# Layer norm scales by GpSimd's power, and a rearranged beginning, in a feed-forward, attention, feed-forward kernel

## The chip, the cores and the metric

One core of a Trainium2 chip runs the program. Its engines work side by side, each through its own queue in order: TensorE (PE, with its weight loads as PEld), VectorE (DVE), ScalarE (ACT), GpSimd (POOL) and SyncE (SP), which here issues all DMAs. The metric is the device time of one execution in microseconds (us), lower is better; the number quoted is the median of several runs.

## What is computed

2048 tokens of width 512 pass through a feed-forward, attention with 16 heads of 32, and the same feed-forward again, each behind a layer norm without learned scale and added to its input:

```python
def _layernorm(x, axis=-1, eps=1e-05):
    m = jnp.mean(x, axis=axis, keepdims=True)
    v = jnp.var(x, axis=axis, keepdims=True)
    return (x - m) / jnp.sqrt(v + eps)

x = x + 0.5 * _L0_ffn_ref(_layernorm(x), gate_W_packed, gate_scales, up_W_packed, up_scales, down_W_packed, down_scales)
x = x + _L0_attn_ref(_layernorm(x), w_qkv, b_qkv, w_out, b_out)
x = x + 0.5 * _L0_ffn_ref(_layernorm(x), ...)
```

The feed-forward is `gelu(x Wg) * (x Wu)` times `Wd`, with 4096 hidden units; its weights come as 4-bit codes with a scale for each 32 of them and are dequantized in the kernel. Attention is causal, with a softmax over float32 scores.

## The kernel before

All of `x` lies in SBUF as 16 tiles of 128 tokens by 512 (`xs`), in four blocks of four tiles. A norm belongs to a block (`norm_steps`): on DVE two instructions per tile for the moments (L88, L89); then, for the four tiles at once, the root on ACT (L95), its reciprocal on DVE (L96) and, where ACT normalizes, a bias on DVE (L98). Then tile by tile: the normalization (`xn`) on ACT (L105) or, for the second feed-forward's first two blocks, on DVE (L107); four PE transposes into a PSUM tile (L115); an ACT copy into `xT` (L116). `xn` has two buffers, so a tile waits for the transposes of the one two before it. Twelve norms run: four in each of the three phases.

ACT holds one table of functions at a time. Root, gelu and exp need different ones, so a root among gelus or exps costs a table load ahead of it and one behind it (ACT_TABLE_LOAD in the profile). `root`, a warm-up at the very beginning (L74), loads the root's table.

The order of the instructions is written out by hand; each engine runs its own in program order.

- The beginning (`ffn`, phase 1): SP loads block 0 of `x`, the gate codes and scales, block 1 of `x`, the up codes and scales, then blocks 2 and 3. DVE takes block 0's moments, the gate dequantization (ten steps, L194 to L190), block 1's moments, the up dequantization, and the four token sums (L256 to L259), which need `xT` of blocks 0 and 1. Behind each dequantization POOL makes four sums of the weights (L234 to L237). The products are Strassen-like: seven products of half-size blocks (L276, in the order 1, 2, 6, 7, 5, 4, 3), whose third needs a token sum and a weight sum.
- During the products the next weights are dequantized in the background: `pump` puts two steps behind each product of the first slot (L194 onward). DVE also evacuates most products (L318 to L336), ACT copies two (L315, L327) and applies gelu (L296), POOL adds one pair (L330).
- Blocks 2 and 3 of a feed-forward are normed during the second half of the first group of hidden units, spread over the products by `paced`; the order of PE is product, four transposes, product, and so on. In both feed-forwards this is the same code.
- At the end of the first feed-forward the last down product (L375, `down_pieces`) is mixed with the norm of attention's blocks 0 and 1 (`norms_behind`): first eight POOL sums (`run(fill[0])`, L360 to L363), then a piece of the product, a group of norm steps, a piece, and so on. A piece's results are added to `x` by DVE (L383) and POOL (L389).
- Attention begins with POOL memsets (L542 to L570) and the norms of blocks 2 and 3, mixed with the first projections (L586). Its last pair of heads carries the second feed-forward's norms of blocks 0 and 1, put between the steps by `extra`; there ACT works on exps (L822, L824), DVE on output additions (L628) and reciprocals (L765), POOL on causal masks (L816) and `attnT` (L768).

Of the kernel before, what the change touches and what calls it, by code (L numbers as in the profile page):

```python
# [9 lines left out]
F32 = mybir.dt.float32  # L10
# [4 lines left out]
AF = mybir.ActivationFunctionType  # L15
ALU = mybir.AluOpType
AX = mybir.AxisListType

P = 128
# [5 lines left out]
NB = S // 512  # L25
# [3 lines left out]
EPS = 1e-5  # L29
# [5 lines left out]
def macaron_kernel(ctx: ExitStack, tc: tile.TileContext, x, packed, scales, wqk, bqk, wv, bv, wo, bo, out):  # L35
# [6 lines left out]
    nc = tc.nc  # L42
    PSUM = bass.MemoryType.PSUM

    const = ctx.enter_context(tc.tile_pool(name="const", bufs=1))
# [14 lines left out]
    xs = [xpair[t // 2][:, t % 2, :] for t in range(NT)]  # L60

    def load_x(tb):
        for t in range(4 * tb, 4 * tb + 4):
            nc.sync.dma_start(out=xs[t], in_=x[t * P : (t + 1) * P, :])
# [2 lines left out]

    ident = const.tile([P, P], F32, tag="ident", name="ident")
    make_identity(nc, ident)
    eps = const.tile([P, 1], F32, tag="eps", name="eps")  # L70
    nc.gpsimd.memset(eps, EPS)

    root = const.tile([P, 1], F32, tag="root", name="root")
    nc.scalar.activation(root, eps, AF.Sqrt)  # L74

    def norm_steps(phase, tb, t_out, temp, on_act=False):

        nm = f"{phase}_{tb}"
        mv = small.tile([P, 4, 2], F32, tag="mv", name=f"mv_{nm}")
        rstd = small.tile([P, 4], F32, tag="rstd", name=f"rstd_{nm}")
        nbias = small.tile([P, 4], F32, tag="nbias", name=f"nbias_{nm}")

        def moments(i):
            st = small.tile([P, 6], F32, tag="st", name=f"st_{nm}_{i}")
            nc.vector.bn_stats(out=st, in_=xs[4 * tb + i])  # L88
            nc.vector.bn_aggr(out=mv[:, i, :], in_=st)  # L89

        def stats(i):
            moments(i)
            moments(i + 1)
            if i == 2:
                nc.scalar.activation(rstd, mv[:, :, 1], AF.Sqrt, bias=eps)  # L95
                nc.vector.reciprocal(rstd, rstd)  # L96
                if on_act:
                    nc.vector.scalar_tensor_tensor(nbias, mv[:, :, 0], -1.0, rstd, ALU.mult, ALU.mult)  # L98

        xn = [None] * 4  # L100

        def normalize(i):
            xn[i] = temp(f"xn_{nm}_{i}")
            if on_act:
                nc.scalar.activation(xn[i], xs[4 * tb + i], AF.Identity, bias=nbias[:, i : i + 1], scale=rstd[:, i : i + 1])  # L105
            else:
                nc.vector.tensor_scalar(  # L107
                    xn[i], xs[4 * tb + i], mv[:, i, 0:1], rstd[:, i : i + 1], ALU.subtract, ALU.mult
                )

        def transpose(i):
            xnv = xn[i].rearrange("t (jc p b) -> t jc b p", jc=2, b=2)
            pt = ps_one.tile([P, 4, P], F32, tag="one", name=f"pt_{nm}_{i}")
            for k in range(4):
                nc.tensor.transpose(pt[:, k, :], xnv[:, k // 2, k % 2, :], ident)  # L115
            nc.scalar.copy(t_out[:, :, i * P : (i + 1) * P], pt)  # L116

        steps = [lambda i=i: stats(i) for i in (0, 2)]
        for i in range(5):
            if i < 4:  # L120
                steps.append(lambda i=i: normalize(i))
            if i > 0:
                steps.append(lambda i=i: transpose(i - 1))
        return steps
# [17 lines left out]
    def ffn(phase, finish, behind, loads, ready=(), first_w=None):  # L142
# [8 lines left out]
        with tc.tile_pool(name=f"w{phase}", bufs=1) as wp, tc.tile_pool(name=f"dq{phase}", bufs=1) as dq, tc.tile_pool(  # L151
            name=f"act{phase}", bufs=1
# [94 lines left out]
            xT, xsum = {}, {}  # L247

            def token_sums(tp):
                eng = nc.vector  # L250
                b1, b2 = xT[2 * tp], xT[2 * tp + 1]
                t = xsum[tp] = wp.tile([P, 3, 2, 512], F32, tag=f"xsum{tp}", name=f"xsum_{phase}_{tp}")
                b11, b21, b12, b22 = b1[:, 0:2, :], b1[:, 2:4, :], b2[:, 0:2, :], b2[:, 2:4, :]
                t3, t2, t4 = [t[:, i] for i in range(3)]
                return [
                    lambda: eng.tensor_tensor(t3, b22, b12, ALU.subtract),  # L256
                    lambda: eng.tensor_tensor(b12, b12, b11, ALU.subtract),
                    lambda: eng.tensor_tensor(t2, b22, b12, ALU.subtract),  # L258
                    lambda: eng.tensor_tensor(t4, b21, t2, ALU.subtract),  # L259
                ]  # L260
# [179 lines left out]
            def run(steps):  # L440
                for f in steps:
                    f()
# [4 lines left out]
            for tb in range(NB):  # L447
                xT[tb] = ready[tb] if tb < len(ready) else x_transposed(f"f{phase}", tb)
            norms = [
                norm_steps(f"f{phase}", tb, xT[tb], normed, True) if tb >= len(ready) else [] for tb in range(NB)  # L450
            ]
            rows = Rows(0, 0, first_w)
            second = Rows(0, 1)
            if phase == 1:
                rows.load(0)
                load_x(1)
                rows.load(1)
                load_x(2)
                load_x(3)
                run(norms[0][:2])  # L460
                gate, up = rows.steps(0), rows.steps(1)
                run(gate[:4])
                run(norms[0][2:])
                run(gate[4:])
                run(norms[1][:2])
                run(up[:4])
                run(norms[1][2:])
                run(up[4:10])
                run(token_sums(0))
                run(up[10:])  # L470
                for m in range(2):
                    second.load(m)
                    background += second.steps(m)
                rows.keep()
            else:
                run(token_sums(0))
# [54 lines left out]
    def attention(xT, xT_f, wqk_wv, next_w):  # L531
        with tc.tile_pool(name="aw", bufs=1) as aw, tc.tile_pool(name="qk", bufs=1) as qkp, tc.tile_pool(
# [43 lines left out]
            for tb in (2, 3):  # L576
                xT.append(x_transposed("a", tb))
                norms += norm_steps("a", tb, xT[tb], normed, True)
# [312 lines left out]
            for p in range(NPAIR):  # L891
# [9 lines left out]
                if p + 1 == NPAIR:  # L901

                    o2, o3 = project_out(2), project_out(3)
                    fills = [o2[:4], o2[4:8], o2[8:12] + o3[:4], []]
                    for i in range(4):
                        extra.setdefault(STARTS[3] + 1 + 2 * i, []).append(o3[4 + i])
                    for tb in range(2):
                        xT_f.append(x_transposed("f2", tb))
                        steps = norm_steps(
                            "f2", tb, xT_f[tb], lambda nm: an.tile([P, D], F32, tag="xn", name=nm)  # L910
                        )
                        for i, step in enumerate(steps):
                            extra.setdefault(STARTS[3] + (2 + i if tb == 0 else 9 + i // 2), []).append(step)
# [61 lines left out]
    def load_first():  # L975
        early["ffn"] = weights("w_2_0_0")
        nc.sync.dma_start(out=early["ffn"], in_=kept[0, 0])

    ffn(1, lambda *_: None, norms_behind, load_qkv)
    attention(xT_a, xT_f, early["qkv"], load_first)  # L980

    def store_out(t, half, x_):

        rows = out[t * P : (t + 2) * P, half * 256 : half * 256 + 256]
        nc.sync.dma_start(out=rows.rearrange("(j p) n -> p j n", p=P), in_=x_)

    ffn(2, store_out, lambda temp: [], lambda: None, xT_f, early["ffn"])


# [62 lines left out]
```

## Time and profile before

| | |
|---|---|
| runs of the kernel | median 3295.95 us of 3 (3295.63, 3295.95, 3298.71) |
| the profiled execution | 3300.15 us, of which the span is 3298.4 us |
| PE busy | 3249.1 us (99%) |
| DVE, ACT, POOL busy | 2043.7 (62%), 872.9 (26%), 1128.3 us (34%) |
| table loads on ACT | 17, of 1.28 us each |
| roots on ACT (L95) | 12, of 0.30 us each |
| reciprocals and biases on DVE (L96, L98) | 12 of 0.18 us and 10 of some 0.16 us |
| normalizations on ACT (L105) | 40, of 0.81 us each |

The profile comes from one execution. Times in the prediction are from the start of its span. A row of a timeline gives the start, the duration (from the first to the last where several are merged), engine, line, operation, output and inputs, shapes, the count, and in brackets how long the engine stood idle before it and whose instruction ended that. In a list of waits each row gives the waiting instructions, whom they waited for, the total, how often, and the longest. Windows give the busy time of each engine in a stretch of the span, and then the clock that was granted to PE as a share of its full clock.

### The profile page before, as it was taken

The numbers are of one execution on the slowest core, as the hardware profiler recorded it, in microseconds if no ns is written. First come the engines' busy times: TensorE is split into PE (matmuls) and PEld (weight loads), VectorE is DVE, ScalarE is ACT, GpSimd is POOL, SyncE is SP. The second block draws the span as 40 slices with busy tenths as digits, with TensorE's granted clock in tenths as the row PEclk, the third lists the DMA queues.
The fourth block names the chain that finished last, engine by engine and source line by source line (L and its number), as shares of the span: only waits on it lengthen the run. The fifth ranks groups of instructions, "written<-read, shape, count | busy, mean of one in ns | idle before, by whom it ended". The sixth has DMA issues, their size and how long they took to land.

```text
span 3298.4 us, 34148 instructions
## 1 busy us (share of the span) xinstructions
PE 3249.1 (99%) x12656; PEld 1723.4 (52%) x12656; DVE 2043.7 (62%) x3152; ACT 872.9 (26%) x1802; POOL 1128.3 (34%) x1319
## 2 busy tenths in 40 slices
PE   7999999999999999999999999999999999999999
PEld 3556565655656565333344333346565565656556
DVE  7877777877777556565655664554455455545545
ACT  4111111111111131554544455431111111111111
POOL 2546464554646341322212223113132221313222
PEclk9999999999999999999999999999999999999999
DMA  3111111111111100000000000100011101011101
GB/s 134 54 65 64 64 47 66 67 48 68 64 64 46 70 17 7 6 15 6 14 3 8 29 21 8 48 23 31 37 45 45 45 23 45 27 41 45 45 23 51
DMA packets 42055, 134.15 MB, mean 41 GB/s; under 512 B 5864, under 2 KB 26344, under 8 KB 35360
## 3 DMA queue, kind: packets, MB, share of 16 engines
q1 hardware_dynamic: 41888, 131.96, 11.0%
q8 instruction: 100, 1.64, 0.2%
q14 instruction: 67, 0.55, 0.1%
HBM read 81.91 MB, written 48.46 MB: 40 GB/s over the span
## 4 chain that ended last, share of the span: by engine, by line
PE 94%; DVE 3%; ACT 2%; issue 1%; POOL 0%; DMA 0%; SPq 0%; POOLq 0%; DVEq 0%; ACTq 0%
PE po L375 23%; PE pu L276 23%; PE pg L276 22%; PE av L729 8%; PE pm L668 6%; PE pqk L586 3%; PE ps L790 2%; PE pp L625 2%; PE pv L603 2%; PE ps L799 2%; ACT pt L822 1%; DVE st_f L88 0%; PE pt_f L115 0%; PE pt_a L115 0%; DVE parts L683 0%
## 5 line engine op out<-in xcount | busy, mean ns | idle before, releaser
L375 PE MATMUL po<-wd,inter 128*128 128x256 f32 x2048 | 484.0, 380 | 0.0
L276 PE MATMUL pg<-xT_f,w 128*128 128x512 f32 x1024 | 479.6, 596 | 0.0
L276 PE MATMUL pu<-xT_f,w 128*128 128x512 f32 x1024 | 476.0, 592 | 0.0
L375 PEld LDWEIGHTS po<-wd,inter 128*128 128x128 f32 x2048 | 389.9, 191 | 155.5 <-issue 104.3
L683 DVE TENSOR_REDUCE parts<-pm 128x1 f32<-128x512 f32 (+3 forms) x640 | 370.9, 608 | 155.0 <-PE pm L668 145.3
L330 POOL TENSOR_TENSOR u<-u,u 128x512 f32<-128x512 f32 x128 | 163.4, 1276 | 865.8 <-ACT u L327 861.5
L389 POOL TENSOR_TENSOR x<-x,d 128x512 f32<-128x512 f32 x248 | 329.7, 1340 | 344.7 <-DVE d L383 170.8
L276 PE MATMUL pg<-xsum,w 128*128 128x512 f32 x768 | 357.4, 595 | 5.2 <-DVE xsum L258 3.2
L375 PE MATMUL po<-wd,s 128*128 128x256 f32 x1536 | 362.2, 379 | 0.0
L276 PE MATMUL pu<-xsum,w 128*128 128x512 f32 x768 | 355.7, 592 | 0.0
L375 PEld LDWEIGHTS po<-wd,s 128*128 128x128 f32 x1536 | 291.5, 190 | 116.2 <-issue 79.2
L668 PE MATMUL pm<-kT,qT 32*128 32x512 f32 (+3 forms) x1280 | 333.9, 574 | 0.5 <-DVE parts L683 0.4
L729 PE MATMUL av<-pt,vaug 128*64 128x512 f32 (+3 forms) x1280 | 304.2, 559 | 4.2 <-ACT both L738 1.9
L822 ACT ACTIVATE pt<-ps 128x512 f32<-128x512 f32 (+3 forms) x576 | 271.5, 532 | 137.4 <-PE ps L799 135.5
L276 PEld LDWEIGHTS pg<-xT_f,w 128*128 128x128 f32 x1024 | 195.8, 192 | 194.6 <-issue 180.9
L276 PEld LDWEIGHTS pu<-xT_f,w 128*128 128x128 f32 x1024 | 194.0, 190 | 189.9 <-issue 180.3
L799 PE MATMUL ps<-qT,kT 32*128 32x512 f32 (+3 forms) x1280 | 277.5, 534 | 0.0
L276 PEld LDWEIGHTS pg<-xsum,w 128*128 128x128 f32 x768 | 146.2, 191 | 152.9 <-issue 140.9
L276 PEld LDWEIGHTS pu<-xsum,w 128*128 128x128 f32 x768 | 145.5, 190 | 142.4 <-issue 135.4
L383 DVE SCALAR_TENSOR_TENSOR x<-po,x 128x512 f32<-128x512 f32 x192 | 131.5, 685 | 115.7 <-ACT d L397 85.9
L816 POOL TENSOR_SCALAR_AFFINE_SELECT pt<-pt 128x256 f32<-128x256 f32 x128 | 52.1, 407 | 388.0 <-ACT pt L815 387.8
L383 DVE SCALAR_TENSOR_TENSOR d<-po,d 128x512 f32<-128x512 f32 x192 | 131.8, 686 | 83.4 <-PE po L375 82.6
(128 smaller groups left out, 3603.6 us busy)
## 6 DMA issues: line engine op xcount, KB each, us to landing
kept<-wd SPq DMA_DIRECT2D x8, 1792.0 KB
wd<-kept SPq DMA_DIRECT2D x8, 1792.0 KB
x<-in_x SPq DMA_DIRECT2D x16, 256.0 KB
pk<-in_gate_codes SPq DMA_DIRECT2D x16, 256.0 KB
sc<-in_gate_scales SPq DMA_DIRECT2D x32, 128.0 KB
pk<-in_up_codes SPq DMA_DIRECT2D x16, 256.0 KB
sc<-in_up_scales SPq DMA_DIRECT2D x32, 128.0 KB
pk<-in_down_codes SPq DMA_DIRECT2D x16, 256.0 KB
```

Source lines behind the costliest of these rows:

```text
L276: nc.tensor.matmul(ps, lhsT=a[:, j, :], rhs=b[:, j, :], start=(j == 0), stop=(j == 1))
L330: nc.gpsimd.tensor_tensor(u4, u4, u2, ALU.add)
L375: nc.tensor.matmul(ps[:, j, :], lhsT=a[i][:, k, bass.ts(2 * q + j, P)], rhs=b[i][:, k, :], start=(k == 0), stop=(k == 1),)
L383: stt(dst, ps, 0.5, other, ALU.mult, ALU.add)
L389: adder.tensor_tensor(dst, dst, other, ALU.add)
L586: nc.tensor.matmul(ps, lhsT=w[:, j, k, :], rhs=xT[tb][:, k, :], start=(k == 0), stop=(k == 3))
L603: nc.tensor.matmul(ps[:, i, :], lhsT=xT[t // 4][:, k, (t % 4) * P : (t % 4 + 1) * P], rhs=wv_sb[:, k, bass.ts(half, 256)], start=(k == 0), ...
L668: nc.tensor.matmul(ps[a][:, :n], lhsT=q[r, bass.ts(4 * g + i, P)], rhs=k[r, kb * 512 : kb * 512 + n], start=True, stop=not on_pe,)
L683: nc.vector.tensor_reduce(parts[:, a, i, kb : kb + 1], ps[a][:, :n], AX.X, ALU.max)
L729: nc.tensor.matmul(av[64 * a : 64 * a + 64, off:], lhsT=vaug[:, c, p % 4, HD * a : HD * a + 2 * HD], rhs=pt[:, a, off:], start=(c == 0), s ...
L799: nc.tensor.matmul(ps[a][:, off:], lhsT=k[r, bass.ts(c, P)], rhs=q[r, g * 512 + off : (g + 1) * 512], start=False, stop=True,)
L822: nc.scalar.activation(pt[:, a, plain:], ps[a][:, plain:], AF.Exp, scale=scale)
```

## The change

The root on ACT and the reciprocal and bias on DVE become four operations on POOL: variance plus epsilon, that to the power -0.5 (against a constant tile `expo`), the mean times -1, and that times the scale. Where DVE normalizes, only the first two. `eps`, `root` and its warm-up go. For blocks 0 and 1 of the first feed-forward tiles 1 and 3 are normalized on POOL, with one instruction of two scalars from a tile, tiles 0 and 2 still on ACT. In the beginning block 1 of `x` is loaded ahead of the gate codes; the moments and scales of both blocks come first, then both blocks' normalizations and transposes, then the gate dequantization, the token sums and the up dequantization.

```diff
-    eps = const.tile([P, 1], F32, tag="eps", name="eps")
-    nc.gpsimd.memset(eps, EPS)
-    root = const.tile([P, 1], F32, tag="root", name="root")
-    nc.scalar.activation(root, eps, AF.Sqrt)
-    def norm_steps(phase, tb, t_out, temp, on_act=False):
+    expo = const.tile([P, 4], F32, tag="expo", name="expo")
+    nc.gpsimd.memset(expo, -0.5)
+    def norm_steps(phase, tb, t_out, temp, on_act=False, on_pool=()):
...
             if i == 2:
-                nc.scalar.activation(rstd, mv[:, :, 1], AF.Sqrt, bias=eps)
-                nc.vector.reciprocal(rstd, rstd)
+                nc.gpsimd.tensor_scalar(rstd, mv[:, :, 1], EPS, None, ALU.add)
+                nc.gpsimd.tensor_tensor(rstd, rstd, expo, ALU.pow)
                 if on_act:
-                    nc.vector.scalar_tensor_tensor(nbias, mv[:, :, 0], -1.0, rstd, ALU.mult, ALU.mult)
+                    nc.gpsimd.tensor_scalar(nbias, mv[:, :, 0], -1.0, None, ALU.mult)
+                    nc.gpsimd.tensor_tensor(nbias, nbias, rstd, ALU.mult)
...
             xn[i] = temp(f"xn_{nm}_{i}")
-            if on_act:
+            if i in on_pool:
+                nc.gpsimd.tensor_scalar(
+                    xn[i], xs[4 * tb + i], rstd[:, i : i + 1], nbias[:, i : i + 1], ALU.mult, ALU.add
+                )
+            elif on_act:
                 nc.scalar.activation(xn[i], xs[4 * tb + i], AF.Identity, bias=nbias[:, i : i + 1], scale=rstd[:, i : i + 1])
...
-                norm_steps(f"f{phase}", tb, xT[tb], normed, True) if tb >= len(ready) else [] for tb in range(NB)
+                norm_steps(f"f{phase}", tb, xT[tb], normed, True, (1, 3) if tb < 2 else ())
+                if tb >= len(ready) else []
+                for tb in range(NB)
...
             if phase == 1:
+                load_x(1)
                 rows.load(0)
-                load_x(1)
                 rows.load(1)
                 load_x(2)
                 load_x(3)
-                run(norms[0][:2])
                 gate, up = rows.steps(0), rows.steps(1)
-                run(gate[:4])
-                run(norms[0][2:])
-                run(gate[4:])
-                run(norms[1][:2])
-                run(up[:4])
-                run(norms[1][2:])
-                run(up[4:10])
-                run(token_sums(0))
-                run(up[10:])
+                run(norms[0][:2] + norms[1][:2] + norms[0][2:] + norms[1][2:])
+                run(gate + token_sums(0) + up)
```

## The prediction

> **What bounds the kernel now.** I read the page's chain first: PE holds 94% of it, so only microseconds in which PE stands still, or runs at half clock, can be won or lost. The waits of PE say for whom it stands:
>
> ```profile
> engine line waited for: us in total, times, longest us
> PE pt_f L115 <- ACT xn_f L105: 24.8, 6, 9.6
> PE ps L790 <- ACT pt L822: 4.5, 4, 2.6
> PE pg L276 <- DVE xsum L258: 3.2, 3, 1.3
> PE pt_a L115 <- ACT xn_a L105: 3.0, 2, 2.8
> ```
>
> All but the third are layer norm (the second is an exp queued behind a root). So I took the timelines around the six places where a norm runs: the start; blocks 2, 3 of the first feed-forward (60 us); attention's blocks 0, 1 (1180 us) and 2, 3 (1210 us); the second feed-forward's 0, 1 (2080 us) and 2, 3 (2160 us). From PE's:
>
> ```profile
> 65.66 1.13 PE L115 MATMUL pt_f<-ident,xn_f 128*128 128x128 f32 x4 [4.95 <-ACT xn_f L105]
> ...
> 1181.87 0.77 PE L115 MATMUL pt_a<-ident,xn_a 128*128 128x128 f32 x4 [2.79 <-ACT xn_a L105]
> ...
> 1209.80 0.63 PE L115 MATMUL pt_a<-ident,xn_a 128*128 128x128 f32 x4
> ...
> 2082.12 0.86 PE L790 MATMUL ps<-wo_bo,ones_b 3*128 3x512 bf16 x2 [2.63 <-ACT pt L822]
> ...
> 2163.99 1.13 PE L115 MATMUL pt_f<-ident,xn_f 128*128 128x128 f32 x4 [4.29 <-ACT xn_f L105]
> ```
>
> The bracket is what PE lost. The windows of DVE, then of all engines (fifth pair of columns POOL, then the clock):
>
> ```profile
> 24.80:65.30 40.50, 38.62 (x65) 0.97 0.33 128
> ```
> ```profile
> 2124.80:2126.90 2.10, 0.12 (x2) 0.07 (x1) 2.03 (x3) 0.41 (x1) 0.00 (x0) 1.00 1.00 430
> ...
> 2127.90:2131.30 3.40, 3.40 (x6) 1.34 (x5) 1.42 (x3) 0.63 (x1) 0.00 (x0) 0.51 1.00 430
> ```
>
> The first: from the token sums until block 3's bias DVE works 38.62 of 40.5 us, so DVE, not PE (which runs dry at 60.7), sets when block 2's norm comes. The others: a stop of PE of 2.0 us is followed by 3.4 us at half clock, a loss of 1.7.
>
> **The change.** It removes 12 roots, the `root` warm-up and 13 of 17 table loads (1.28 us each) from ACT, 12 reciprocals and 10 `nbias` from DVE, and four normalizations from ACT; POOL gets 44 tiny operations and those four. Each norm waits for a POOL chain of four (two for `xT_f` blocks 0, 1). POOL's tiny two-input operation (L697, 128x8) takes 0.21 us, the cast L694 0.22; a power is not in this trace. Bounds: 0.21, and 1.34 (the mean 128x512 addition, L389). I take 0.3, near the tiny row: a chain is 0.22+0.3+0.22+0.21 and gaps of 0.06, 1.1 us (1.0 to 2.2). A one-input 128x512 on POOL: affine selects take 0.29 at 128x128, 0.407 at 128x256, so 0.64 by extension; bounds 0.52 (memset of 128x512) and 1.34. I take 0.7.
>
> *Start and blocks 2, 3 of the first feed-forward.* Three transfers (codes, two scales) go behind four of `x` on SP; 1 MB at the 295 GB/s of 2 to 4 us is 3.6 us, and the codes are now wanted at 11.3 instead of 8.5 us, so this hides. DVE does block 1's four moments right behind block 0's (7.88 + 4 x 0.8 and some landing = 11.3). On POOL both chains stand ahead of the first normalization, so it waits for block 1's moments: 12.5 us. Two buffers then make a zigzag: POOL 0.7, transposes 0.75, POOL 0.7, transposes 0.75, copy 0.6, ACT 0.8, transposes 0.7, copy 0.6, ACT 0.8, two transposes 1.35, copy 0.6, with some 0.9 of hops: the sums can begin at 21.75 instead of 24.82. But the dequantization of `up` (as 8.54 to 14.44: 5.9 us) now follows the sums: 21.75 + 4 x 1.23 + 0.3 for POOL's clashes + 5.9 = 32.9, where DVE reached the background work at 31.02 before. That is 1.9 late. POOL's sums of `up` move onto DVE's background work (about 0.5 more); block 2's root, reciprocal and bias (58.99 to 59.76) go: -0.8. L329, which feeds the gelu ahead of block 2's normalization on ACT, starts at 61.98+1.6 = 63.6; 0.69 + 0.63 + 0.80 and hops bring the transposes to 65.9, against 65.66. ACT without four table loads saves some 0.4 in the next two. PE, 3 us earlier into the first product, only waits longer. Term: -0.2 (-2 to +3 by the bounds above).
>
> *Attention 0, 1.* POOL takes everything in order, and there the changed kernel's order has eight sums and an addition ahead of the chain:
>
> ```profile
> 1181.02 1.51 ACT L105 ACTIVATE xn_a<-x,nbias_a,rstd_a 128x512 f32<-128x512 f32 x2
> ```
> ```profile
> 1182.14 1.27 POOL L363 TENSOR_TENSOR s<-inter,s 128x512 f32<-128x512 f32 x1
> 1183.37 1.71 POOL L389 TENSOR_TENSOR x<-x,d 128x512 f32<-128x512 f32 x1
> ```
>
> The moments are ready at 1176.2; POOL is free at 1183.41+1.34 = 1184.75, the chain ends at 1185.85, ACT's 0.81 brings the transposes to 1186.75 instead of 1181.87: +4.9 (4.5 to 6). Behind PE's waiting transposes stand all later pieces of the down product; nothing covers it. The half clock after the stop (1182.4 to 1185.8, 0.51) is there in both.
>
> *Attention 2, 3.* The chain stands behind 16 memsets:
>
> ```profile
> 1206.75 2.40 POOL L570 MEMSET vaug<- 128x128 f32 x16
> ```
>
> They end at 1209.15; with 1.1 and 0.81 the transposes come at 1211.2 instead of 1209.80: +1.4. A new stop may bring half a clock: 1.7 at one chance in three, +0.5. Term +1.9 (1 to 3.1). Here the page "TensorE: Matmul & The Clock Gate", section "HAM oscillation", speaks of idle gaps above some 3.4 us only; the 2.0 us stop above disagrees. By that rule this half microsecond would fall away and the sum would be -1.8.
>
> *Second feed-forward 0, 1, inside attention.* ACT's queue holds exps behind a root that waits for moments:
>
> ```profile
> 2074.36 1.28 ACT L95 ACT_TABLE_LOAD   x1
> 2079.87 0.30 ACT L95 ACTIVATE rstd_f<-mv_f,eps 128x4 f32<-128x4 f32 x1 [4.22 <-DVE mv_f L89]
> 2080.18 1.28 ACT L822 ACT_TABLE_LOAD   x1
> ```
>
> Without it PE's 2.63 and the half clock behind it (2083.5 to 2087.0, 0.51: 1.7) go: -4.3. POOL's two operations end at 2080.5, hidden by DVE's L765; but the next output piece then waits some 0.7 for POOL's `attnT`. At block 1 ACT's 0.23 and 0.17 go, and perhaps half of another 1.7: -1.0; DVE's 0.92 stays (0.55 for root and reciprocal, 0.65 for POOL's pair). Term -4.6 (-6.5 to -2.5).
>
> *Second feed-forward 2, 3.* DVE is not full there. Moments end at 2157.3, POOL's chain at 2158.5; L329, without the reciprocal's 0.76, at 2159.55; 0.69+0.63+0.80 and hops: transposes at 2161.7 instead of 2163.99, -2.3. The slow stretch of 4.9 us (clock 0.50) shrinks to one of 3.4: -0.7, and the next transposes wait 0.3 less. Term -3.3 (-4.7 to -1.5).
>
> **Sum.** -0.2+4.9+1.9-4.6-3.3 = -1.3 us. The profiled execution spans 3298.4 (3300.15 with what lies around it), so it would span 3297.1; the runs' median is 4.2 below it, 3295.95, and I put the same difference on it: 3294.6. Elementwise work belongs on VectorE by the page "GPSIMD Engine Reference", section 4.1, which calls one-input work on GpSimd roughly line rate; its 769 ns for 512 elements (section 3.1) would add an estimated 0.1 to the sum.
>
> **Rivals.** A measurement of this kernel can tell about 0.2%, 6.6 us.
> (1) Slower: the power is dear on POOL. The chain lies open at the start (through DVE's queue), at 1185, at 1210 and twice near 2090; at 2158 it has 2 us of cover. Each microsecond above 1.1 costs 5, and from 2.7 us per chain (7.9/5 more) it decides. At 3 us: -1.3+9.5 = +8.2, 3304. For it: no row shows a power. Against: four columns only, and POOL's tiny rows take 0.2.
> (2) Faster: DVE gives way, because its 38.62 us hold clashes with POOL (L202 1.64 instead of 0.69) that the new order dissolves; then the 3.1 us at the start stay (-3.7 with the reciprocal), and the shorter stops end the half clock at 60 and 2160 us: 2 x 1.7. -1.3-3.7-3.4 = -8.4, 3287.5. Against: POOL gets more work in just that stretch.
> (3) The table loads were covered: in the second feed-forward the next wait takes half of the 7.9 back; +2.6, 3298.6. For it: PE's 0.92 for DVE and `attnT` are near.
> (4) It doesn't do what it says: four table loads stay, by the changed kernel's own order, so a root is left nowhere; no chance given.
>
> **How the numbers follow.** Forecast 0.71, (1) 0.11, (2) 0.12, (3) 0.06. The terms' ends added are -7.7 and +8.1, all at once unlikely; the range of 8 in 10 reaches 3288 to 3302. Beyond 6.6 us lie most of (1) and (2) and a little of the forecast's own ends: faster 0.13, within 0.77, slower 0.10.
>
> **What would show it.** The first token sum (DVE `xsum`) near 21.7 and the first transposes of `xn_f` block 2 near 66 us: the DVE step. PE's wait for `xn_a` near 7.7 us, its longest after the start's and block 2's: the POOL step. No `ps` wait for ACT near 2080, and the block 2 stop of the second feed-forward near 2 us. Wrong if POOL's power takes over 1.5 us, or if `xn_a` waits under 4.

## The result, and the profile after

Run by turns with the kernel before on one chip, the changed kernel takes 3303.24 us in the median of 14 runs (3300.27 to 3305.55), the one before 3297.44 of 14 (3294.49 to 3300.43). The ratio is 1.0017 (95% interval 1.0010 to 1.0024): 5.8 us slower, inside the 0.2% named as the bound and just outside the predicted range (3288 to 3302), on the other side of "before" than the forecast. Of the 8.6 us by which it misses the 3294.6 forecast, 1.5 are the base: the forecast stood on a median before of three runs, 3295.95. Against before, -1.3 was forecast. The profiled execution after took 3303.2 us (span 3301.3).

Below are the waits of PE in the profile after: waiting instruction, whom it waited for, us in total, how often, the longest.

```profile
engine line waited for: us in total, times, longest us
PE pt_f L117 <- ACT xn_f L107: 23.6, 5, 11.1
PE pt_a L117 <- ACT xn_a L107: 11.2, 3, 8.9
PE pt_f L117 <- POOL xn_f L103: 4.0, 2, 3.5
...
PE pt_f L117 <- DVE xn_f L109: 2.1, 2, 1.8
PE ps L787 <- ACT pt L819: 1.4, 1, 1.4
```

The exp's wait (`ps`, 4.5 us in four) has shrunk to 1.4, attention's wait (`pt_a`, 3.0) has grown to 11.2. The single stops, from PE's timeline after (start, duration, engine, line, operation, in brackets the idle time before):

```profile
69.97 1.13 PE L117 MATMUL pt_f<-ident,xn_f 128*128 128x128 f32 x4 [8.69 <-ACT xn_f L107]
...
1192.72 1.13 PE L117 MATMUL pt_a<-ident,xn_a 128*128 128x128 f32 x4 [8.89 <-ACT xn_a L107]
...
1224.03 0.74 PE L117 MATMUL pt_a<-ident,xn_a 128*128 128x128 f32 x4 [2.12 <-ACT xn_a L107]
...
2106.81 0.72 PE L117 MATMUL pt_f<-ident,xn_f 128*128 128x128 f32 x4 [1.82 <-DVE xn_f L109]
...
2167.34 0.75 PE L117 MATMUL pt_f<-ident,xn_f 128*128 128x128 f32 x4 [1.91 <-ACT xn_f L107]
```

So the losses sit at the first feed-forward's block 2 (8.69 against 4.95) and at attention's block 0 (8.89 against 2.79), the gains in the second feed-forward. The operation that no row showed before, from the costliest groups of instructions (busy us, mean ns of one):

```profile
L93 POOL TENSOR_TENSOR rstd_f<-rstd_f,expo 128x4 f32<-128x4 f32 x8 | 8.8, 1094 | 0.7
...
L93 POOL TENSOR_TENSOR rstd_a<-rstd_a,expo 128x4 f32<-128x4 f32 x4 | 4.2, 1039 | 0.3
L103 POOL TENSOR_SCALAR xn_f<-x,rstd_f,nbias_f 128x512 f32<-128x512 f32 x4 | 3.9, 987 | 5.3 <-PE pt_f L117 2.7 <-issue 2.6
```

A power of four columns costs 1.04 us, not 0.3; a normalization on POOL 0.99 in the mean, not 0.7. The timeline of POOL at the start, after, shows both, and their order:

```profile
11.40 0.31 POOL L92 TENSOR_SCALAR rstd_f<-mv_f 128x4 f32<-128x4 f32 x1 [1.22 <-DVE mv_f L86]
11.80 1.47 POOL L93 TENSOR_TENSOR rstd_f<-rstd_f,expo 128x4 f32<-128x4 f32 x1
13.33 0.64 POOL L95 TENSOR_SCALAR nbias_f<-mv_f 128x4 f32<-128x4 f32 x1
14.05 0.34 POOL L96 TENSOR_TENSOR nbias_f<-nbias_f,rstd_f 128x4 f32<-128x4 f32 x1
14.38 1.27 POOL L103 TENSOR_SCALAR xn_f<-x,rstd_f,nbias_f 128x512 f32<-128x512 f32 x1
17.01 1.15 POOL L103 TENSOR_SCALAR xn_f<-x,rstd_f,nbias_f 128x512 f32<-128x512 f32 x1 [1.36 <-PE pt_f L117]
19.50 0.77 POOL L103 TENSOR_SCALAR xn_f<-x,rstd_f,nbias_f 128x512 f32<-128x512 f32 x1 [1.34 <-PE pt_f L117]
```

Block 1's chain takes 3.0 us while DVE dequantizes (until 17.5), 1.92 where DVE leaves POOL alone; only then comes block 0's tile 1 on POOL (14.38). DVE, before and then after:

```profile
24.82 1.27 DVE L256 TENSOR_TENSOR xsum<-xT_f 128x1024 f32<-128x1024 f32 x1 [0.61 <-ACT xT_f L116]
...
31.02 0.41 DVE L194 TENSOR_SCALAR mag<-pk 128x512 uint32<-128x512 uint32 x1
```
```profile
25.54 1.47 DVE L258 TENSOR_TENSOR xsum<-xT_f 128x1024 f32<-128x1024 f32 x1 [8.03 <-ACT xT_f L118]
...
31.12 0.42 DVE L196 TENSOR_SCALAR mag<-pk 128x512 uint32<-128x512 uint32 x1
...
36.94 0.42 DVE L196 TENSOR_SCALAR mag<-pk 128x512 uint32<-128x512 uint32 x1
```

After the change DVE stands idle for 8.03 us before the first token sum, then still has the `up` dequantization (31.12) to do, and reaches the background work at 36.94, against 31.02 before. And POOL ahead of attention's norm, after:

```profile
1188.55 1.26 POOL L391 TENSOR_TENSOR x<-x,d 128x512 f32<-128x512 f32 x1
1189.90 0.23 POOL L92 TENSOR_SCALAR rstd_a<-mv_a 128x4 f32<-128x4 f32 x1
1190.20 1.04 POOL L93 TENSOR_TENSOR rstd_a<-rstd_a,expo 128x4 f32<-128x4 f32 x1
1191.31 0.23 POOL L95 TENSOR_SCALAR nbias_a<-mv_a 128x4 f32<-128x4 f32 x1
1191.62 0.20 POOL L96 TENSOR_TENSOR nbias_a<-nbias_a,rstd_a 128x4 f32<-128x4 f32 x1
```

The chain stands behind POOL's last addition, without a gap: it waits for its turn, not for its data (DVE's last moments of this block end at 1181).

### The profile page after: what moved, and what is told of

It is laid out like the page before. It is cut to its first block, busy times and chain, and to the rows that moved or that the text cites. A ratio compares the mean times of both kernels' runs of the same rounds, so it can differ in the third digit from the quotient of the medians.

```text
span 3301.3 us, 34144 instructions
## 1 busy us (share of the span) xinstructions
PE 3242.5 (98%) x12656; PEld 1722.5 (52%) x12656; DVE 2037.6 (62%) x3130; ACT 848.9 (26%) x1772; POOL 1152.7 (35%) x1367
## 3 DMA queue, kind: packets, MB, share of 16 engines
q8 instruction: 100, 1.64, 0.2%
## 4 chain that ended last, share of the span: by engine, by line
PE 94%; DVE 2%; POOL 1%; ACT 1%; issue 1%; DMA 0%; POOLq 0%; SPq 0%; DVEq 0%; ACTq 0%
PE pu L278 23%; PE pg L278 23%; PE po L377 23%; PE av L726 8%; PE pm L665 6%; PE pqk L583 3%; PE ps L787 2%; PE pp L622 2%; PE pv L600 2%; PE ps L796 2%; ACT pt L819 1%; PE pt_f L117 0%; DVE st_f L85 0%; DVE parts L680 0%; PE pt_a L117 0%
```

## The experiments

The theory before the runs: the new beginning costs several microseconds by itself, because DVE gets through the start later; in attention the order of POOL's sums costs as much; the power only its own microsecond where it lies open. The rival: it is the power. The median of each run against the kernel before on its own chip (3297.21 us of 33 runs for the first four, 3297.93 of 27 for the others):

| kernel | median us | against before | ratio, 95% |
|---|---|---|---|
| old_beginning | 3294.97 | -2.2 | 0.9993 (0.9984 to 1.0002) |
| new_beginning_root | 3302.46 | +5.3 | 1.0016 (1.0007 to 1.0025) |
| cheap_power | 3295.53 | -1.7 | 0.9996 (0.9987 to 1.0004) |
| sums_split | 3296.87 | -0.3 | 1.0000 (0.9991 to 1.0009) |
| no_pool_norm | 3299.78 | +1.9 | 1.0007 (0.9998 to 1.0016) |
| sums_last | 3298.83 | +0.9 | 1.0003 (0.9995 to 1.0012) |
| moments_first | 3296.08 | -1.9 | 0.9994 (0.9985 to 1.0003) |
| best | 3284.37 | -13.6 | 0.9960 (0.9948 to 0.9973) |

Against before, only new_beginning_root and best are clear of noise; the other six intervals contain 1. Against the changed kernel (1.0010 to 1.0024), old_beginning, cheap_power, sums_split, moments_first and best are clear of it. What no_pool_norm and sums_last show rests on their profiles alone.

Microseconds of this size are better read by stage. From PE's timeline of each profiled execution I took where five marks lie and subtracted: S1 from the start to the first gate product (`pg`) behind block 3's transposes, S2 from there to attention's first projection (`pqk`), S3 to its first score maximum (`pm`), S4 to the first product of the second feed-forward, S5 to its first gate product behind block 3's transposes. The rest is 1114.4 us in all. Differences to before; the last column is DVE's reaching the background work, then the start of block 2's transposes:

| kernel | S1 | S2 | S3 | S4 | S5 | DVE free, transposes |
|---|---|---|---|---|---|---|
| before, us | 85.46 | 1117.47 | 15.70 | 902.66 | 62.67 | 31.02, 65.66 |
| after | +4.75 | +7.20 | +2.40 | -8.62 | -2.75 | 36.94, 69.97 |
| old_beginning | -3.60 | +7.14 | +2.41 | -8.56 | -2.74 | 31.32, 63.96 |
| new_beginning_root | +4.53 | -0.02 | 0.00 | -2.20 | -0.73 | 34.59, 70.01 |
| cheap_power | +3.07 | +5.93 | +1.55 | -9.50 | -4.48 | 36.27, 69.31 |
| sums_split | +3.52 | +1.95 | +2.41 | -8.60 | -2.77 | 36.75, 69.79 |
| no_pool_norm | -0.13 | +6.45 | +4.11 | -7.08 | -4.45 | 32.95, 66.00 |
| sums_last | -2.32 | +6.64 | +4.10 | -7.20 | -2.77 | 32.67, 65.24 |
| moments_first | -4.55 | +6.65 | +4.11 | -6.91 | -4.43 | 30.66, 63.00 |
| best | -2.21 | -3.63 | +2.54 | -8.65 | -2.75 | 31.85, 63.87 |

A stretch of half clock is 3.4 us long or a multiple of it, and 3.4 us of it cost up to 1.7. Before's profiled execution has one at 1418.0 us that no other of the first five has, so about 1.7 of each S4 there is not the change's. No_pool_norm, sums_last and moments_first have one in S3 and one near 1425: that is the 1.4 to 1.7 by which their S3 and S4 lie above after's. Where S5 is -4.4 or -4.5, after's stretch at 2133.8 or at 2168.0 is absent. Each kernel has one profiled execution, and where such a stretch falls differs from one to the next (last section): differences of 1.7 us or less in a single stage are weak evidence.

**old_beginning.** The power stays; loads, order and engines of the beginning as before.

```diff
-                norm_steps(f"f{phase}", tb, xT[tb], normed, True, (1, 3) if tb < 2 else ())
+                norm_steps(f"f{phase}", tb, xT[tb], normed, True, ())
...
+                rows.load(0)
                 load_x(1)
-                rows.load(0)
                 rows.load(1)
...
+                run(norms[0][:2])
                 gate, up = rows.steps(0), rows.steps(1)
-                run(norms[0][:2] + norms[1][:2] + norms[0][2:] + norms[1][2:])
-                run(gate + token_sums(0) + up)
+                run(gate[:4])
+                run(norms[0][2:])
+                run(gate[4:])
+                run(norms[1][:2])
+                run(up[:4])
+                run(norms[1][2:])
+                run(up[4:10])
+                run(token_sums(0))
+                run(up[10:])
```

> The power stays on GpSimd in every norm; the beginning alone is as before (loads, order, all normalizations on ScalarE). Theory: the loss of the first 90 us (+4.8) is the order, the token sums ahead of the up dequantization, so that VectorE stands idle 8 us. Then block 2's transposes of the first feed-forward come near 64 us (before 65.7, changed 70.0) and the time is 6 to 7 us below the changed kernel, near 3297. Rival: the power of 1.04 us in each norm is the loss; then the beginning gains at most 2 and the time stays above 3301.

Measured -2.2 us against before where after has +5.8: the new beginning costs 8. In the stages it is S1 alone (-3.60 against +4.75). From its PE timeline:

```profile
63.96 0.74 PE L117 MATMUL pt_f<-ident,xn_f 128*128 128x128 f32 x4 [1.92 <-ACT xn_f L107]
```

The stop is 1.92 us instead of 8.69, and no half clock follows it. It came 2 us below the expected 3297; the 10.2 us of half clock behind block 2 in after are gone too.

**new_beginning_root.** The new beginning and its POOL tiles, the scales by root, reciprocal and bias as before.

```diff
-                nc.gpsimd.tensor_scalar(rstd, mv[:, :, 1], EPS, None, ALU.add)
-                nc.gpsimd.tensor_tensor(rstd, rstd, expo, ALU.pow)
+                nc.scalar.activation(rstd, mv[:, :, 1], AF.Sqrt, bias=eps)
+                nc.vector.reciprocal(rstd, rstd)
                 if on_act:
-                    nc.gpsimd.tensor_scalar(nbias, mv[:, :, 0], -1.0, None, ALU.mult)
-                    nc.gpsimd.tensor_tensor(nbias, nbias, rstd, ALU.mult)
+                    nc.vector.scalar_tensor_tensor(nbias, mv[:, :, 0], -1.0, rstd, ALU.mult, ALU.mult)
```

> The other half alone: the new beginning, with two tiles per block normalized by GpSimd, but root, reciprocal and bias where they were before. Theory: the beginning's loss of 4 to 5 us stays (block 2's transposes near 69), attention's blocks 0, 1 go back to a stop of 2.8 us and its blocks 2, 3 to none, the stop at the exps of 2.6 us comes back: about 4 above before, near 3301.5. Rival (the power is the loss at the start too): within 1.5 of before.

+5.3 us, S1 +4.53: the beginning loses without any power in it. S2 and S3 stand at zero: what attention loses is the chain of four on POOL. The token sums, from DVE's timeline of this run, begin 2.2 us earlier than in the changed kernel, and still 1.6 behind the 21.75 of the prediction:

```profile
23.35 1.73 DVE L260 TENSOR_TENSOR xsum<-xT_f 128x1024 f32<-128x1024 f32 x1 [4.74 <-ACT xT_f L120]
```

**cheap_power.** A product in place of the power; the kernel leaves out the true scale, so only its times can be read.

```diff
-                nc.gpsimd.tensor_tensor(rstd, rstd, expo, ALU.pow)
+                nc.gpsimd.tensor_tensor(rstd, rstd, expo, ALU.mult)
```

> The changed kernel with the power replaced by a multiplication of the same two tiles: the scale is not computed, so the output is not the reference's. It prices the power by itself. Each chain falls from 1.95 to about 1.1, which is what was forecast for it. Theory: 1.2 us back at the start, 0.8 at 1190, 0.8 at 1221, 1 in the second feed-forward's blocks 0, 1, nothing in its blocks 2, 3: 3.8 in all, near 3299.4. Rival (only the power was mis-sized, everything else of the forecast holds): 8 back, near 3295.

-1.7 us, 7.5 below after: by the time alone the rival's number. By the rows only part of it is direct. One of its products on POOL, then the stop of PE at attention's block 0:

```profile
1188.54 0.20 POOL L93 TENSOR_TENSOR rstd_a<-rstd_a,expo 128x4 f32<-128x4 f32 x1
```
```profile
1190.21 1.13 PE L117 MATMUL pt_a<-ident,xn_a 128*128 128x128 f32 x4 [8.05 <-ACT xn_a L107]
```

The product takes 0.20 us for 1.04, and where the chain lies open the wait shrinks by about that: block 2's transposes come 0.66 earlier, attention's stop falls from 8.89 to 8.05, S3 by 0.85, the wait for DVE in the second feed-forward's block 1 from 1.82 to 0.98; 3.2 us. The profiled execution is 6.4 us shorter than after's (span 3294.9). Of the other 3.2, some 2.7 are half clock behind stops that are no shorter than after's: behind block 2 (8.69 us in both) 6.8 us of it are left of 10.2, and the stretch at 2133.8, behind a stop of 1.98 in after and 1.99 here, is absent. So the cheap product doesn't show that the power costs 7.5. And the token sums, on DVE, still start late:

```profile
25.12 1.23 DVE L258 TENSOR_TENSOR xsum<-xT_f 128x1024 f32<-128x1024 f32 x1 [8.28 <-ACT xT_f L118]
```

DVE idles even longer (8.28 us): little of the beginning's delay is the power's.

**sums_split.** Half of the eight sums behind the scales of attention's blocks 0 and 1.

```diff
-            run(fill[0])
+            run(fill[0][:4])
             groups = behind(normed)
+            if phase == 1:
+                groups[3] += fill[0][4:]
```

> The changed kernel, but the last four of GpSimd's eight sums at the end of the first feed-forward are issued behind the scales of attention's blocks 0 and 1 instead of ahead of them. Theory: the stop of 8.9 us there is the queue of sums ahead of the chain; it falls to about 3.2, the slow clock behind it gets shorter by 1, and the time falls by 6 to 7, near 3296.5. Rival: the later down pieces wait for the moved sums instead, and less than 3 comes back.

-0.3 us, 6.1 below after. S2 falls from +7.20 to +1.95; that S1 falls too, by 1.2, is a shorter stretch of half clock behind block 2 (6.8 us, not 10.2), ahead of the edit. PE's timeline:

```profile
1186.18 1.13 PE L117 MATMUL pt_a<-ident,xn_a 128*128 128x128 f32 x4 [3.58 <-ACT xn_a L107]
```

The stop shrinks by 5.31, close to four sums of POOL (4 x 1.35, start to start); the half clock behind it does not (PE works 6.0 us at half speed after the stop; in after 5.9, from 1192.72 to 1198.6). So the order of the sums is a second loss, separate from the beginning's.

**no_pool_norm** and **sums_last** take the beginning apart: all tiles on ACT, and the `up` dequantization ahead of the token sums.

```diff
-                norm_steps(f"f{phase}", tb, xT[tb], normed, True, (1, 3) if tb < 2 else ())
+                norm_steps(f"f{phase}", tb, xT[tb], normed, True, ())
```
```diff
-                run(gate + token_sums(0) + up)
+                run(gate + up[:10] + token_sums(0) + up[10:])
```

> The changed kernel with all normalizations of the beginning on ScalarE again (GpSimd keeps the scales). Theory: GpSimd's 1.27 and 1.15 us under VectorE's dequantization and the zigzag through two buffers hold the token sums back; they come near 23 instead of 25.5 us, the beginning loses some 2 instead of 4.75, near 3300. Rival: the order alone is the loss and ScalarE's turn is as long; then the sums come at 25 or later and nothing changes.

> The changed kernel with one move: the up dequantization ahead of the token sums, where VectorE stood idle for 8 us. Theory: VectorE reaches the background work near 31 instead of 36.9 us and is not behind; block 2's transposes come near 64 instead of 70, the beginning ends 6 earlier, near 3296.5. Rival: the token sums are late anyway and PE's wait for the third product eats it; less than 2.

From DVE's timeline of no_pool_norm, and then of sums_last:

```profile
22.20 1.23 DVE L258 TENSOR_TENSOR xsum<-xT_f 128x1024 f32<-128x1024 f32 x1 [5.09 <-ACT xT_f L118]
...
32.95 0.42 DVE L196 TENSOR_SCALAR mag<-pk 128x512 uint32<-128x512 uint32 x1
```
```profile
26.20 1.55 DVE L258 TENSOR_TENSOR xsum<-xT_f 128x1024 f32<-128x1024 f32 x1 [2.39 <-ACT xT_f L118]
...
32.67 0.94 DVE L196 TENSOR_SCALAR mag<-pk 128x512 uint32<-128x512 uint32 x1
```

Without POOL's normalizations the sums start 3.3 us earlier, though the slow chain of block 1 is still there (11.24 to 14.39): ACT has block 0's tiles to do meanwhile. With the `up` dequantization ahead, the idle 8.03 become 2.39. Either way DVE is free some 4 us earlier, and the transposes of block 2 come 4.0 and 4.7 earlier. Sums_last came out 2.3 us above its number, which the two stretches of half clock (S3, S4) more than explain; its transposes came at 65.24, not at 64.

**moments_first.** Both edits; what is left of the new beginning is the loads and the moments first.

> Both of these together: the moments of both blocks first, all normalizations on ScalarE, up dequantization ahead of the token sums. Theory: they add, to a point: token sums near 23, block 2's transposes near 62, near 3294.5. Rival: one of them makes the other worthless, within 1 of the run with the sums last.

-1.9 us, 1.6 above the number, again with the two stretches. S1 is -4.55, the best of all; with up's dequantization ahead DVE no longer stands idle for the sums, which start at 24.52. DVE is free at 30.66, so the two savings (3.99 and 4.27) overlap: together 6.28.

**best.** old_beginning, with the sums four by four behind the scales of attention's blocks 0 and 1, and the `vaug` memsets behind the norms of blocks 2 and 3.

```diff
-            run(fill[0])
             groups = behind(normed)
+            if phase == 1:
+                groups[1] += fill[0][:4]
+                groups[3] += fill[0][4:]
+            else:
+                run(fill[0])
...
-            for t in range(NT):
-                nc.gpsimd.memset(vaug[:, t, :, HD : 2 * HD], 1.0)
...
+            for t in range(NT):
+                nc.gpsimd.memset(vaug[:, t, :, HD : 2 * HD], 1.0)
             fill = qk[4:6] + v[:2] + qk[6:8] + v[2:]
```

> The power on GpSimd in all norms with the beginning of before, and two moves of what GpSimd has queued: of the eight sums at the end of the first feed-forward four go behind the scale of attention's block 0 and four behind that of block 1, and the memsets of vaug go behind the norms of its blocks 2 and 3. Theory: the beginning 3.6 below before, the stop of 2.8 at attention's blocks 0, 1 falls to under 0.5 and its slow clock goes (-4), blocks 2, 3 lose 1.1 instead of 2.4, the second feed-forward's 9 stay: 14 to 15 below before, near 3283. Rival: the moved sums stop the later pieces by as much as they free, and it ends at old_beginning's 3295.

3284.37 us (five runs, 3282.47 to 3285.97), ratio 0.9960 (0.9948 to 0.9973): below both kernels, and 10.6 below old_beginning, which differs in the two moves alone; S2 goes from +7.14 to -3.63. PE's timeline, then POOL's:

```profile
1176.96 0.74 PE L117 MATMUL pt_a<-ident,xn_a 128*128 128x128 f32 x4
...
1180.37 1.99 PE L377 MATMUL po<-wd,s 128*128 128x256 f32 x8 [0.47 <-POOL s L364]
...
1206.37 0.74 PE L117 MATMUL pt_a<-ident,xn_a 128*128 128x128 f32 x4 [2.25 <-ACT xn_a L107]
```
```profile
1174.12 0.23 POOL L92 TENSOR_SCALAR rstd_a<-mv_a 128x4 f32<-128x4 f32 x1 [0.28 <-DVE mv_a L86]
1174.43 1.04 POOL L93 TENSOR_TENSOR rstd_a<-rstd_a,expo 128x4 f32<-128x4 f32 x1
...
1203.52 0.23 POOL L92 TENSOR_SCALAR rstd_a<-mv_a 128x4 f32<-128x4 f32 x1 [1.69 <-DVE mv_a L86]
```

The stop at attention's start is gone and with it the half clock; the price is 0.47 us for a sum that comes late. The memsets' move was a miss: the chain now waits for DVE's moments (1.69) and the stop is 2.25 instead of 2.12. S1 came at -2.21, not at the expected -3.6, with one stretch of half clock at 64.7 that old_beginning hasn't. The beginning of moments_first together with this order was not tried.

## Why the prediction was wrong

The terms, each as predicted and as the stages show it:

| term | predicted | measured |
|---|---|---|
| start and blocks 2, 3 of the first feed-forward | -0.2 (-2 to +3) | +4.75 |
| attention 0, 1 | +4.9 (4.5 to 6) | +7.2 |
| attention 2, 3 | +1.9 (1 to 3.1) | +2.4 |
| second feed-forward 0, 1 | -4.6 (-6.5 to -2.5) | -8.6, some -6.9 without before's stretch at 1418 |
| second feed-forward 2, 3 | -3.3 (-4.7 to -1.5) | -2.75 |
| sum | -1.3 | +3.0, some +4.7 without that stretch |

**The step that failed** is "Two buffers then make a zigzag ... the sums can begin at 21.75": they began at 25.54. Of the 3.8 us late, 1.9 lie ahead of POOL's first normalization (14.38, not 12.5: block 1's chain took 3.0 us, not 1.1), 1.0 in the two of its normalizations that the zigzag counts (1.27 and 1.15 for 0.7 each), the remaining 0.9 in transposes, copies and hops. The runs agree: the sums begin at 23.35 with the chains off POOL, at 22.20 with the normalizations off it, at 25.12 with the power alone made cheap. I had seen that POOL takes both chains first and had priced chain and tiles as if POOL were alone, although my own figures had DVE dequantizing at that time. The step after it held: from the token sums to the background work 11.4 us, worked out as 11.15. So did "DVE, not PE, sets when block 2's norm comes": block 2's transposes follow 32.0 to 33.1 us behind DVE's being free in the eight kernels without roots, and 34.6 and 35.4 in the two with them. The prediction's own numbers (65.9 and 32.9) put 33.0 there, and after has 33.03. So the root's removal gave what was worked out for it, 1.6 us, and the whole miss of the transposes (69.97 for 65.9) is the 5.9 us by which DVE came late instead of 1.9. "PE, 3 us earlier into the first product" fell with the same step: that product came at 24.73, and at 23.96 before. The longer stop then brought 10.2 us of half clock instead of 6.8, some 0.8 of the term (5.6 us of work at half speed instead of 4.0).

**The power was mis-sized**: 1.04 us, not 0.3, a chain of 1.92 instead of 1.1. "Near the tiny row" was the wrong choice between the bounds 0.21 and 1.34. Rival (1) named this mechanism and its price per place; its point of 2.7 us per chain was not reached, so it alone did not decide. Neither of the prediction's signs of being wrong came (a power over 1.5 us, a wait for `xn_a` under 4); among its signs of being right the first token sum and block 2's transposes missed. Worked by its own rule it is 5 x 0.82 = 4.1 us, against 3.2 read directly.

**Attention 0, 1**: the mechanism was right (POOL's queue, the longest wait after the start's, sums_split and best), the size 2.3 short: 0.8 the power, 0.4 POOL's additions, and 1.2 half clock. "The half clock after the stop ... is there in both" took it for equally long: PE works 5.9 us at half speed behind the longer stop, 3.4 before.

**Attention 2, 3** held, with a stop of 2.12; the slow stretch put at one chance in three followed a stop of 2.12 to 2.25 in three kernels of seven, and not in after; which three is told in the last section.

**Second feed-forward 0, 1** gained more than I thought: the stretches at 2083.6 and 2100.6 went both and whole, where I had counted half of the second, and the 0.7 for a late `attnT` did not show. Together with the stop of 2.63 that is 6.0 of the 6.9; the remaining 0.9 I have not traced. Only that stop of the exps' 4.5 us stood behind a root, which is what the sum had used: one of 1.46 at 2037 is there in all ten kernels. Blocks 2, 3 came as worked out: 1.91 for a stop, instead of the expected 2.

Rival (2), DVE giving way, fell: the 1.64 us row went, but others came (`val<-mag`, L202 after, takes 1.37 us twice where 0.43 is usual), and the start was slower, not faster. Rival (3), covered table loads, fell: the wait for DVE in block 1 grew from 0.92 to 1.82, and cheap_power's 0.98 shows that this is the power; nothing else there took the place of the exp's. The loads themselves went as the order said, 4 left of 17.

## What to carry to other kernels

When work goes to another engine, ask first what stands ahead of it in that engine's queue at that place: the power cost 1.0 to 1.5 us wherever it ran, but its place made a stop of 8.9 in attention, and a reordering of the same instructions took that to nothing. Reading ahead in the start is worth something only if the engine that sets the pace gets through sooner: here the token sums came 0.7 us later than before, and DVE, with a dequantization still behind them, 5.9. And for a short operation of a kind that the trace does not show, leave the forecast open as far as the far bound: this one came at 1.04 us between 0.21 and 1.34.

## What the runs showed of the hardware

- POOL's power of 128x4 elements takes 1.04 us where a product of the same shape takes 0.20. Beside DVE's dequantization POOL's operations stretch (in after, at the start): the power to 1.47, L95's tiny multiplication from 0.23 to 0.64, the 128x512 normalization from 0.77 to 1.27. The Trainium skill's "GPSIMD Engine Reference", section 3.1, gives 769 ns for 512 elements, which the undisturbed rows meet, and section 8 speaks of contention with DVE's instructions in a two-port mode or of two SBUF inputs; by the figure alone all four normalizations would take 0.77, and the first two took 1.27 and 1.15.
- Half clock comes in steps of 3.41 us (3.4, 6.8, 10.2, in new_beginning_root 13.7), and the steps keep to a grid through the whole execution: in after they begin at 65.36, 1188.35, 2051.92, 2133.84 and 2167.97, which lie 329, 253, 24 and 10 times 3.4133 us apart.
- In these runs what follows a short stop goes not by its length alone but mostly by how it lies on this grid. The stop at attention's blocks 2, 3 lies whole in one step in no_pool_norm (2.13 us), sums_last (2.12) and moments_first (2.13), and half clock begins with the next step. In after, old_beginning, sums_split and best the border of a step divides it, the longer part being 1.55, 1.63, 1.48 and 1.61 us, and none follows. The stop of 2.0 us between 2110 and 2135 (1.98 in after) lies whole in one step and is followed in nine kernels; in cheap_power it is divided (1.10 and 0.89), and is not. This isn't the whole rule: a stop of 1.92 that lies whole in a step at 2159.0 of moments_first is not followed, where one of 1.91 is in six others, and one of 1.45 near 2040 is followed in nine kernels of ten. Windows of no_pool_norm, then of after (PE's, PEld's, DVE's, ACT's and POOL's busy time, the granted clock of PE, DMA share and GB/s):

```profile
1219.40:1222.80 3.40, 3.40 (x5) 1.35 (x4) 0.00 (x0) 1.42 (x3) 0.13 (x1) 0.50 0.00 0
```
```profile
1224.00:1229.00 5.00, 4.97 (x21) 3.07 (x22) 0.00 (x0) 3.19 (x6) 0.99 (x3) 1.00 0.00 0
```

"TensorE: Matmul & The Clock Gate" of the Trainium skill, section "What's actually happening", describes a window of 3413 ns that runs freely, which these steps fit; its warning of gaps above some 3.4 us (section "HAM oscillation") does not cover a stop of 2 us with half clock behind it.
